# Seven strips of a convolution layer: small steps of a norm and a count moved behind the first half of the strip's vertical sums

## The chip, the core and the metric

The kernel runs on one core of a Trainium2 chip. The metric is the device time of one execution in microseconds; lower is better. All tensors are 32-bit floats. Engines are named as in the profile: PE (TensorE, matrix products, writes to PSUM), DVE (VectorE), ACT (ScalarE), POOL (GpSimd) and SP (SyncE, which here only issues DMAs).

## The reference

Two layers, each of the form x + conv(groupnorm(x)), on x of shape (2, 128, 256, 256). Layer 0's "convolution" is a dilated halo attention over 8x8 windows. Layer 1, to which the change belongs, is

```python
t1 = conv(x, w1, 5x1 kernel, padding 2 rows)        # 128 channels to 128, along the rows
t3 = depthwise conv(t1, w3, 3x1 kernel, padding 1)
t2 = unfold(x, width taps 0, 2, 4)                  # dilated by 2 along the columns
t4 = einsum('nckhw,ckg->nghw', t2, w4)              # g = 8
t5 = t4[:, None] * t3.reshape(n, c // g, g, h, w)
x  = x + t5
```

The group norm ahead of it has 32 groups of 4 channels and needs mean and variance over the whole image before the first row can be normalised.

## The kernel before

The 128 channels lie on the 128 partitions. Both layers go through the image in strips of 8 rows: 32 strips an image, 64 in all, numbered k. Layer 0 (`attention_fast`) writes its result x1 to device memory, strip by strip, and collects the statistics of x1 for layer 1's norm on the way. Layer 1 (`convolutions_fast`, L607) starts when layer 0 ends.

Two small pieces of work are left over when layer 1 starts. **The norm of image 1** (`Norms.steps`, L115): the statistics of its last strips come at the very end of layer 0, so its mean and reciprocal deviation are computed inside layer 1, in seven steps, each ended by a `yield`: `bn_aggr` on DVE (L119); a matmul `pm` that averages over each group (L122); the mean and three one-column operations on DVE (L125 to L130); a matmul `pv` (L133); one DVE operation (L136); a square root on ACT (L139); five one-column DVE operations (L143 to L148). They are needed only when the second image starts, at strip 31. **The count** (`in_range`, L882): one reduction and a memset on DVE in its first part, one matmul `total` and a cast on DVE in its second. It says whether all softmax denominators were in range; a slower program behind it would run if they were not.

A strip k of layer 1, in program order:

- `load_rows1(k + 2)` (L629): SP issues the loads of x1's rows for the strip after the next into `raw` (six buffers).
- `unfold(k)` (L686): 12 matmuls of PE from the normalised rows `xm` into `g` (L692), copied to SBUF by ACT (L698).
- `first_rows(k)` (L709): ACT carries two rows of `t1` over (L723).
- `start_strip(k + 1)` (L666), which calls `normalise1`: ACT copies the four rows that two strips share (L649); DVE normalises the new eight (L651).
- `vertical(k, 2)` (L727): the 5x1 convolution for half of the strip, in the form of sums and differences of rows: matmuls `a_c` (L706, called from L735), copied by ACT into `both` (L737); `a_d` (L740), added to `both` by DVE into `c` (L744); `a_e` (L706) and `a_o` (L706), added to `c` by DVE (L751 and L757) into `t1`; then ACT starts `t3` (L762). `a_c`, `a_d`, `a_e` and `a_o` rotate through three PSUM buffers, so each needs the one three places back to have been read.
- `row_sums(k + 1)` (L670): ACT carries over one row of `sm` (L677); DVE makes the row sums `sm` (L678) and their differences `df` (L682), which the next strip's `a_c` and `a_d` read.
- `depthwise(k, 2)` (L764): two DVE operations on `t3` (L769).
- `vertical(k, 4)`: the other half, in the same way.
- `spread(k)` (L774): four matmuls into four PSUM banks of one buffer each, b0 to b3 (L780).
- `combine` (L786) on DVE: `y` = bank times `t3`, for b0 and b1; then `depthwise(k, 4)`; then b2 and b3 (L789).
- `finish(k)` (L794): POOL issues a DMA that adds x1 to `y` (L797); SP issues the store of `y` (L798), which waits for it.

The small matmuls `total`, `pm` and `pv` use the tag "b3", so each takes the bank that `combine` of strip k − 1 reads last and that `spread(k)` writes next.

The order is written out by hand: inside `tc.manual_schedule(engines=ORDERED)` each engine, and SP's queue, runs its instructions in the order of the program, and semaphores are put in where one depends on another. So an instruction that waits holds up everything after it on its engine. The loop is at L819; the steps stand in it at L827 to L832:

```python
if k in (1, 2):
    count_good[k - 1](ps_b, "b3")
if k == 2:
    steps = norm.steps(st_y[NB - 1], ps_b, f"y{NB - 1}", "b3")
for _ in range({3: 1, 4: 2, 5: 2, 6: 1, 7: 1}.get(k, 0)):
    next(steps)
```

That is: strip 1 the reduction of the count, strip 2 its matmul and cast, strip 3 `bn_aggr`, strip 4 `pm` and the mean, strip 5 `pv` and the operation after it, strip 6 the square root, strip 7 the rest.

Of the kernel before, what the change touches and what calls it, by code (L numbers as in the profile page):

```python
# [606 lines left out]
def convolutions_fast(tc, io, x1_d, norm, st_y, out, weights, count_good):  # L607
# [4 lines left out]
    with ExitStack() as l1:  # L612
# [16 lines left out]
        def load_rows1(b, s):  # L629

            if s == 0:
                pre = rawp.tile([P, 8, W], F32, tag="raw", name=f"raw1_{b}_pre")
                nc.sync.dma_start(pre[:, 5:8, :], x1_d[b][0][:, 0:3, :])
                raws[b, -1] = pre
            t = rawp.tile([P, 8, W], F32, tag="raw", name=f"raw1_{b}_{s}")
            nc.sync.dma_start(t[:, 0:5, :], x1_d[b][s][:, 3:8, :])
            if s + 1 < NS:
                nc.sync.dma_start(t[:, 5:8, :], x1_d[b][s + 1][:, 0:3, :])
            raws[b, s] = t

        def normalise1(b, s, k, mean, rstd):
            cur, prev = xn[k % 2], xn[(k + 1) % 2]
            if s == 0:
                nc.gpsimd.memset(cur[:, 0:1, :], 0.0)
                nc.vector.tensor_scalar(
                    cur[:, 1:4, 2 : 2 + W], raws[b, -1][:, 5:8, :], mean, rstd, ALU.subtract, ALU.mult
                )
            else:
                nc.scalar.copy(cur[:, 0:4, :], prev[:, 8:12, :])  # L649
            n = 8 if s + 1 < NS else 5  # L650
            nc.vector.tensor_scalar(  # L651
                cur[:, 4 : 4 + n, 2 : 2 + W], raws[b, s][:, 0:n, :], mean, rstd, ALU.subtract, ALU.mult
            )
            if n < 8:
                nc.gpsimd.memset(cur[:, 4 + n : 12, :], 0.0)
# [10 lines left out]
        def start_strip(k):  # L666
            b, s = divmod(k, NS)
            normalise1(b, s, k, *norm.done[f"y{b}"])

        def row_sums(k):  # L670
            s = k % NS
            xt = xn[k % 2]
            sms[k] = sm = tp.tile([P, 5, W], F32, tag="sm", name=f"sm_{k}")
            dfs[k] = df = tp.tile([P, 4, W], F32, tag="df", name=f"df_{k}")
            lo = 0 if s == 0 else 1
            if s > 0:
                nc.scalar.copy(sm[:, 0:1], sms[k - 1][:, 4:5])  # L677
            nc.vector.tensor_tensor(  # L678
                sm[:, lo:5], xt[:, 2 * lo + 1 : 10 : 2, 2 : 2 + W], xt[:, 2 * lo + 2 : 11 : 2, 2 : 2 + W],
                ALU.add,  # L680
            )
            nc.vector.tensor_tensor(df, sm[:, 0:4], sm[:, 1:5], ALU.subtract)  # L682
# [3 lines left out]
        def unfold(k):  # L686

            xt = xn[k % 2]
            pg = ps_pj.tile([P, 512], F32, tag="pj", name=f"g_{k}")
            for tap in range(3):  # L690
                for j in range(4):
                    nc.tensor.matmul(  # L692
                        pg[32 * j : 32 * j + 32, :], w4[:, tap, :],
                        xt[:, 2 * j + 1 : 2 * j + 3, 2 * tap : 2 * tap + W],
                        start=tap == 0, stop=tap == 2,
                    )
            t4 = wk.tile([P, 512], F32, tag="t4", name=f"t4_{k}")
            nc.scalar.copy(t4, pg)  # L698
            t3 = wk.tile([P, 8, W], F32, tag="t3", name=f"t3_{k}")
            y = wk.tile([P, 8, W], F32, tag="y", name=f"y_{k}")  # L700
            ts[k] = t4, t3, y

        def taps(name, n, terms):
            pa = ps_a.tile([P, 512], F32, tag="a", name=f"a_{name}")
            for i, (w, rows) in enumerate(terms):
                nc.tensor.matmul(pa[:, : n * W], w, rows, start=i == 0, stop=i == len(terms) - 1)  # L706
            return pa[:, : n * W].rearrange("p (r w) -> p r w", w=W)

        def first_rows(k):  # L709

            s = k % NS
            xt = xn[k % 2]

            t1s[k] = t1 = tp.tile([P, 10, W], F32, tag="t1", name=f"t1_{k}")
            if s == 0:
                nc.gpsimd.memset(t1[:, 0:1, :], 0.0)
                top = taps(
                    f"{k}_first", 1,
                    [(w1[:, tap], xt[:, tap - 1 : tap, 2 : 2 + W]) for tap in (2, 3, 4)],
                )  # L720
                nc.scalar.copy(t1[:, 1:2, :], top)
            else:
                nc.scalar.copy(t1[:, 0:2, :], t1s[k - 1][:, 8:10, :])  # L723
            if s + 1 == NS:
                nc.gpsimd.memset(t1[:, 9:10, :], 0.0)

        def vertical(k, m):  # L727

            s = k % NS
            xt, sm, df, t1 = xn[k % 2], sms[k], dfs[k], t1s[k]  # L730

            def rows(j):
                return xt[:, j : j + 3 : 2, 2 : 2 + W]

            pa = taps(f"{k}_c_{m}", 1, [(w1s[:, 0], sm[:, m - 1 : m])])  # L735
            both = wk.tile([P, 1, W], F32, tag="both", name=f"both_{k}_{m}")
            nc.scalar.copy(both, pa)  # L737
            pa = ps_a.tile([P, 512], F32, tag="a", name=f"a_{k}_d_{m}")
            for i, w in enumerate((w1[:, 1], w1s[:, 1])):
                nc.tensor.matmul(  # L740
                    pa[:, W * i : W * i + W], w, df[:, m - 2 + i : m - 1 + i], start=True, stop=True
                )
            c = wk.tile([P, 2, W], F32, tag="c", name=f"c_{k}_{m}")
            nc.vector.tensor_tensor(  # L744
                c, pa.rearrange("p (r w) -> p r w", w=W), both.to_broadcast([P, 2, W]), ALU.add
            )
            pa = taps(
                f"{k}_e_{m}", 2,
                [(w, rows(2 * m - 4 + 2 * i)) for i, w in enumerate((w1[:, 0], w1s[:, 2], w1s[:, 3]))],
            )  # L750
            nc.vector.tensor_tensor(t1[:, 2 * m - 2 : 2 * m + 1 : 2, :], pa, c, ALU.add)  # L751
            pa = taps(
                f"{k}_o_{m}", 2,
                [(w, rows(2 * m - 3 + 2 * i)) for i, w in enumerate((w1s[:, 4], w1s[:, 5], w1[:, 4]))],
            )
            n = 1 if m == 4 and s + 1 == NS else 2
            nc.vector.tensor_tensor(  # L757
                t1[:, 2 * m - 1 : 2 * m + 2 * n - 2 : 2, :], pa[:, 0:n], c[:, 0:n], ALU.add
            )
            t3 = ts[k][1]  # L760
            j = 2 * m - 4
            nc.scalar.activation(t3[:, j : j + 4], t1[:, j : j + 4, :], AF.Copy, scale=w3[:, 0:1])  # L762

        def depthwise(k, m):  # L764

            t1, t3 = t1s[k], ts[k][1]
            j = 2 * m - 4
            for tap in (1, 2):
                nc.vector.scalar_tensor_tensor(  # L769
                    t3[:, j : j + 4], t1[:, j + tap : j + tap + 4, :], w3[:, tap : tap + 1],  # L770
                    t3[:, j : j + 4], ALU.mult, ALU.add,
                )
# [41 lines left out]
        with tc.manual_schedule(engines=ORDERED):  # L814
            for k in range(2):
                load_rows1(*divmod(k, NS))
            start_strip(0)
            row_sums(0)
            for k in range(NB * NS):  # L819
                more = k + 1 < NB * NS  # L820
                if k + 2 < NB * NS:
                    load_rows1(*divmod(k + 2, NS))
                unfold(k)
                first_rows(k)


                if k in (1, 2):  # L827
                    count_good[k - 1](ps_b, "b3")
                if k == 2:
                    steps = norm.steps(st_y[NB - 1], ps_b, f"y{NB - 1}", "b3")  # L830
                for _ in range({3: 1, 4: 2, 5: 2, 6: 1, 7: 1}.get(k, 0)):
                    next(steps)  # L832
                if more:
                    start_strip(k + 1)

                vertical(k, 2)
                if more:
                    row_sums(k + 1)
                depthwise(k, 2)
                vertical(k, 4)  # L840
                banks = spread(k)
                combine(k, banks, (0, 1))
                if not more:
                    finish_half(k, 0)
                depthwise(k, 4)
                combine(k, banks, (2, 3))
                if more:
                    finish(k)
                else:
                    finish_half(k, 1)  # L850
# [596 lines left out]
```

## Time and profile before

| What | us |
|---|---|
| Median of 3 runs | 3231.89 (3228.91 to 3233.07) |
| The profiled execution, its time | 3226.79 |
| The profiled execution, its span | 3224.9 |
| PE busy in the span | 3084.4 (96%) |
| DVE busy | 2611.7 (81%) |
| ACT busy | 1440.3 (45%) |
| POOL busy | 586.7 (18%) |
| PE busy in 2100 to 3225 us (layer 1) | 1092.15 of 1125 |
| DVE busy in the same | 975.16 |

The span is from the first to the last instruction of the profiled execution; its time has a little around that. A row of the profile names the line, the engine, what is written and read, how often, the busy time and the mean of one; "idle before" is time in which the engine stood still just before such an instruction, and the name after the arrow is what ended it. Wait rows have the total, the number of times and the longest. PE, the costliest engine, runs matmuls in a pipeline, so consecutive rows overlap a little in the timeline. In layer 1 a first row at about 2104 us is the first `unfold`, and strip 1 starts at 2129.32 us.

### The profile page before, as it was taken

How to read it: one execution, taken by the hardware profiler on the slowest of the kernel's cores; microseconds unless marked ns; L12 is line 12 of the kernel's file. 1: busy time of each engine (PE TensorE's matmuls, PEld its weight loads, DVE VectorE, ACT ScalarE, POOL GpSimd, SP SyncE). 2: the span in 40 equal slices, each digit the busy share in tenths (PEclk: the TensorE clock that was granted, in tenths of full speed). 3: DMA queues.
4: the chain of work that ended last, by engine and by line, in shares of the span. 5: the costliest groups of instructions: out<-in, count | busy, mean ns of one | idle time of the engine just before them, and what ended most of it. 6: DMA issues, size and time to landing. Idle time of an engine off the chain costs nothing.

```text
span 3224.9 us, 117425 instructions
## 1 busy us (share of the span) xinstructions
PE 3084.4 (96%) x53030; PEld 2282.9 (71%) x53030; DVE 2611.7 (81%) x4152; ACT 1440.3 (45%) x2481; POOL 586.7 (18%) x917
## 2 busy tenths in 40 slices
PE   0799999999999999999999999989999999999998
PEld 0688898899988889988998889834444444444443
DVE  8788888888888777777777777678888898888887
ACT  0455555555555555555555555522332323233322
POOL 2222222222222222222222222100000000000001
PEclk9999999999999999999999999999999999999999
DMA  9443333333333222222222222146677767676775
GB/s 396 148 133 111 122 108 111 110 120 119 107 111 99 81 75 80 85 68 86 80 78 85 68 88 81 40 135 160 187 194 182 185 186 190 178 190 186 194 182 153
DMA packets 125116, 426.42 MB, mean 132 GB/s; under 512 B 9024, under 2 KB 75328, under 8 KB 92096
## 3 DMA queue, kind: packets, MB, share of 16 engines
q1 hardware_dynamic: 115536, 352.76, 32.2%
q0 software_dynamic: 9072, 66.06, 11.3%
q8 instruction: 420, 6.88, 0.9%
q14 instruction: 88, 0.72, 0.1%
HBM read 284.57 MB, written 134.22 MB: 130 GB/s over the span
## 4 chain that ended last, share of the span: by engine, by line
PE 76%; issue 18%; DVE 2%; POOL 2%; DMA 1%; ACT 0%; SPq 0%; POOLq 0%; DVEq 0%; ACTq 0%
PE f_pv L416 15%; PE f_pq L341 8%; PE f_s L451 8%; PE f_o L476 8%; PE f_pk L341 7%; PE f_py L341 7%; PE a_e L706 5%; PE a_o L706 5%; PE f_pa L395 4%; PE f_s L435 4%; PE g L692 3%; PE a_d L740 2%; POOL y L797 1%; PE b L780 1%; PE a_c L706 1%
## 5 line engine op out<-in xcount | busy, mean ns | idle before, releaser
L422 DVE COPY f_vt<-f_pv 64x512 f32<-64x512 f32 x512 | 354.3, 694 | 291.6 <-ACT f_vt L422 291.4
L416 PE MATMUL f_pv<-f_wqkvT,f_xn 128*128 128x128 f32 x4096 | 491.4, 278 | 0.0
L416 PEld LDWEIGHTS f_pv<-f_wqkvT,f_xn 128*128 128x128 f32 x4096 | 466.9, 192 | 8.6
L762 ACT ACTIVATE t<-t,w 128x1024 f32<-128x1024 f32 x128 | 147.2, 1150 | 689.0 <-DVE t L757 689.0
L323 POOL COPY f_xq<-f_xn 128x256 f32<-128x256 f32 x512 | 309.7, 649 | 757.8 <-DVE f_xn L309 757.8
L376 ACT ACTIVATE f_q<-f_pq,f_head 128x512 f32<-128x512 f32 x512 | 309.9, 687 | 304.2 <-PE f_pq L341 304.2
L460 ACT ACTIVATE f_p<-f_s 128x512 f32<-128x512 f32 x512 | 264.3, 603 | 404.1 <-PE f_s L451 404.0
L422 ACT COPY f_vt<-f_pv 64x512 f32<-64x512 f32 x512 | 297.4, 582 | 118.0 <-PE f_pv L416 117.8
L769 DVE SCALAR_TENSOR_TENSOR t<-t,w,t 128x1024 f32<-128x1024 f32 x256 | 329.9, 1289 | 7.5 <-ACT t L762 1.3
L451 PEld LDWEIGHTS f_s<-f_q,f_kt 64*64 64x64 f32 x16384 | 250.6, 135 | 49.3 <-issue 49.3
L341 PE MATMUL f_pq<-f_xn,f_wq_s 128*128 128x192 f32 (+2 forms) x1520 | 277.2, 330 | 3.3 <-DVE f_xn L309 2.6
L451 PE MATMUL f_s<-f_q,f_kt 64*64 64x64 f32 x16384 | 268.2, 220 | 0.0
L476 PE MATMUL f_o<-f_vt,f_p 128*32 128x66 f32 x16384 | 265.3, 223 | 0.9 <-DVE mean_x L125 0.3
L797 POOL DMA_DIRECT2D y<-f_x x63 | 71.3, 1131 | 1025.1 <-DVE y L789 960.7
L476 PEld LDWEIGHTS f_o<-f_vt,f_p 128*32 128x32 f32 x16384 | 243.2, 111 | 10.5 <-DVE f_cf L408 1.0
L341 PE MATMUL f_pk<-f_xn,f_wqkvT 128*128 128x256 f32 x1024 | 245.3, 380 | 0.0
L341 PEld LDWEIGHTS f_pq<-f_xn,f_wq_s 128*128 128x128 f32 x1520 | 232.3, 188 | 17.0 <-issue 4.2
L341 PE MATMUL f_py<-f_ot,f_woT 128*128 128x256 f32 x1024 | 241.8, 378 | 2.3 <-DVE f_ot L494 2.3
L706 PE MATMUL a_e<-xm,w1s 128*128 128x512 f32 x512 | 240.7, 591 | 0.0
L706 PE MATMUL a_o<-xm,w1s 128*128 128x512 f32 x512 | 240.5, 590 | 0.0
L300 POOL COPY f_xn<-f_xn 128x1280 f32<-128x1280 f32 x62 | 86.5, 1395 | 772.1 <-PE f_pv L416 772.1
L510 DVE TENSOR_TENSOR f_x<-f_py,f_raw 128x512 f32<-128x512 f32 x256 | 175.9, 687 | 58.7 <-PE f_py L341 50.7
(126 smaller groups left out, 4612.6 us busy)
## 6 DMA issues: line engine op xcount, KB each, us to landing
f_raw<-in_x SPq DMA_DIRECT2D x62, 1280.0 KB, 7.8
f_sx<-in_x SPq DMA_DIRECT2D x64, 1024.0 KB, 7.3
f_x<-f_x SPq DMA_DIRECT2D x128, 512.0 KB, 3.3
y<-f_x POOLq DMA_DIRECT2D x63, 1024.0 KB, 8.2
out<-y SPq DMA_DIRECT2D x63, 1024.0 KB, 4.9
raw<-f_x SPq DMA_DIRECT2D x64, 640.0 KB, 6.4
raw<-f_x SPq DMA_DIRECT2D x62, 384.0 KB, 6.9
f_raw<-in_x SPq DMA_DIRECT2D x2, 1024.0 KB, 6.9
```

Source lines behind the costliest of these rows:

```text
L323: nc.gpsimd.tensor_copy(xq[:, t2, half].rearrange("p t r n c e -> p r t (n c) e"), cells[:, :, 16 * half : 16 * half + 16, 1 + t2 : 9 : 4, ...
L341: nc.tensor.matmul(dst[:, 32 * lo : 32 * hi], w, moving[:, lo:hi], start=True, stop=True)
L376: nc.scalar.activation(q[:, c, :, i], pq.rearrange("p (n x) -> p n x", n=NPAIR), AF.Copy, scale=head[:, i : i + 1],)
L416: nc.tensor.matmul(pv[:, P * n : P * n + P], xn[k % 2][:, r, 4 * j + n].rearrange("p c x -> p (c x)"), wvT, start=True, stop=True,)
L422: (nc.vector.tensor_copy if c else nc.scalar.copy)(vt[rows, 4 * j : 4 * j + 4, :, c, 0:32], pv[rows].rearrange("p (n h d) -> p n h d", n=4 ...
L451: nc.tensor.matmul(sc[g][n // 8][64 * c : 64 * c + 64, n % 8].rearrange("p i x -> p (i x)"), keys_k[rows, c, 48 * n : 48 * n + 64], qs[u][ ...
L460: nc.scalar.activation(pts[u][:, g, 8 * half : 8 * half + 8].rearrange("p n i x -> p (n i x)"), sc[g][half].rearrange("p n i x -> p (n i x ...
L476: nc.tensor.matmul(po[32 * h : 32 * h + 32, n - lo], p[:, h // 2, n, h % 2], vt[:, n, h], start=True, stop=True,)
L510: nc.vector.tensor_tensor(x1[:, :, c:W:2], py.rearrange("p (m t) -> p t m", t=4), raws[k][:, r:8:2, c:W:2], ALU.add,)
L706: nc.tensor.matmul(pa[:, : n * W], w, rows, start=i == 0, stop=i == len(terms) - 1)
L762: nc.scalar.activation(t3[:, j : j + 4], t1[:, j : j + 4, :], AF.Copy, scale=w3[:, 0:1])
L769: nc.vector.scalar_tensor_tensor(t3[:, j : j + 4], t1[:, j + tap : j + tap + 4, :], w3[:, tap : tap + 1], t3[:, j : j + 4], ALU.mult, ALU.add,
```

## The change

The six lines above move from between `first_rows(k)` and `start_strip(k + 1)` to between `vertical(k, 2)` and `row_sums(k + 1)`. In the file it looks as if the two calls moved up; the order of everything else stays. Strips in which no step is run have the same order before and after.

```diff
                 unfold(k)
                 first_rows(k)
+                if more:
+                    start_strip(k + 1)
+
+                vertical(k, 2)
 
 
                 if k in (1, 2):
                     count_good[k - 1](ps_b, "b3")
                 if k == 2:
                     steps = norm.steps(st_y[NB - 1], ps_b, f"y{NB - 1}", "b3")
                 for _ in range({3: 1, 4: 2, 5: 2, 6: 1, 7: 1}.get(k, 0)):
                     next(steps)
-                if more:
-                    start_strip(k + 1)
-
-                vertical(k, 2)
                 if more:
                     row_sums(k + 1)
                 depthwise(k, 2)
```

## The prediction

> **What bounds the kernel now.** I read the page first: PE is busy 96% of the span and makes 76% of the chain that ended last. The edit touches layer 1 only, from about 2100 us on, so I asked next for the busy time of stretches of that layer (columns: PE, PE loads, DVE, ACT, POOL, then granted clock, DMA share, GB/s).
>
> ```profile
> 2166.40:2185.60 19.20, 17.37 (x72) 7.50 (x68) 18.36 (x19) 5.20 (x8) 0.86 (x1) 1.00 0.60 159
> 2185.60:2207.50 21.90, 18.86 (x74) 8.96 (x70) 15.73 (x22) 5.29 (x8) 0.86 (x1) 0.92 0.64 181
> 2300.00:2900.00 600.00, 600.00 (x2409) 274.09 (x2408) 533.29 (x604) 182.50 (x282) 43.69 (x40) 1.00 0.71 185
> ```
>
> From 2300 us PE never rests (600.00 of 600), with DVE at 89%: PE sets the pace there. Only the first strips leave PE idle. The waits of PE in layer 1 say why:
>
> ```profile
> PE g L692 <- issue: 5.4, 1, 5.4
> PE total L893 <- DVE y L789: 3.1, 1, 3.1
> PE pv_y L133 <- DVE y L789: 3.1, 1, 3.1
> PE pm_y L122 <- DVE y L789: 3.0, 1, 3.0
> PE g L692 <- DVE xm L651: 2.6, 1, 2.6
> PE a_c L706 <- DVE c L744: 2.1, 2, 1.7
> ```
>
> The two rows of g are the start of the layer, untouched. The three of 3.1, 3.1 and 3.0 are the small matmuls of the count and the norm. Their target is PSUM bank b3, and DVE reads b3 last of all in the strip before (combine, L789). The timeline around the first, PE (columns: start, us, engine, line, what):
>
> ```profile
> 2146.21 2.79 PE L692 MATMUL g<-xm,w 128*32 128x512 f32 x24
> 2152.07 0.19 PE L893 MATMUL total<-ones,both 128*1 128x1 f32 x2 [3.08 <-DVE y L789]
> 2152.19 0.70 PE L706 MATMUL a_c<-sm,w1s 128*128 128x256 f32 x2
> ```
>
> and DVE, whose last read of b3 is the second of these two:
>
> ```profile
> 2150.73 1.29 DVE L789 TENSOR_TENSOR y<-b,t 128x512 f32<-128x512 f32 x2
> ```
>
> PE is through with unfold at 2149.00; DVE leaves b3 at 2152.02. In strip 1, with no small matmul, PE goes straight from g (ends 2132.11) to a_c (2132.04, overlapped), while DVE is just as far behind (y ends 2135.15).
>
> **Strip by strip.** Unfold (L692) starts, in the timeline, for k = 1 to 10: 2129.32, 2146.21, 2166.36, 2185.61, 2207.52, 2227.76, 2244.81, 2261.68, 2279.53, 2296.48. An undisturbed strip is 16.88. Excess over that: k=2 3.27, k=3 2.37, k=4 5.03, k=5 3.36, k=6 0.17, k=7 0, k=8 0.97, k=9 0.07; together 15.2 us, the ceiling.
>
> **What the Trainium skill says.** "PSUM — Partial Sum Buffer", Engine vs sequencer instructions: matmuls run in program order, the other engines' queues are FIFO. The trace agrees: all of vertical stood behind the waiting `total` for 3.08 us. "TensorE: Matmul & The Clock Gate", What's actually happening: PE's clock falls to half after an idle window of 3413 ns, and windows run freely. The 0.92 above is one: in 2191 to 2196 us the mean clock is 0.66, so (1 − 0.66) × 5 / 0.5 = 3.4 us at half speed, costing 1.7. It follows one of the three waits and not the other two of the same length. "ScalarE: Activation LUTs", What ACT_TABLE_LOAD costs: 1283 ns and about 1380 of drain. The trace shows 1.28 and no drain: load 2231.75, square root 2233.04, the next copy 2233.15, so I take 1.4.
>
> **The change part by part.** Strips without steps (0, 8 and later) keep their order. In 1 to 7 the steps now stand after vertical(k, 2), still ahead of row_sums.
>
> *Count, strips 1 and 2.* In strip 2 the matmul comes after a_o, which in strip 1 ends 6.7 us after the strip's first a_c (2138.76 against 2132.04), when b3 has been free for 3.6 us. The wait of 3.08 and its refill go: 3.27 − 0.12 for the matmul itself (2152.07 to 2152.19) = **3.15**. DVE's cast needs that matmul, 0.28 behind it before; DVE has o's add (L757, 0.69) to do first, so it waits for nothing. The reduction and memset (0.13 of DVE in strip 1) lie in DVE's slack: it waited 0.86 for a_o there. If that cover were gone they cost 0.13.
>
> *pm and pv, strips 4 and 5.* Likewise, leaving 0.24 each (2191.45 to 2191.69). The half clock goes with the wait, as no idle window of that length is left in these strips. Strip 5: 3.36 − 0.24 = **3.1**. Strip 4: 5.03 − 0.24 = **4.8**, of which 1.7 is clock. The four small operations behind pm are 0.66 of DVE; in their place and after o's add, 0.44 of that lies in DVE's old wait for ACT's sm copy (L677), which is waited for in every strip.
>
> *bn_aggr, strip 3.* DVE, 3.61 long:
>
> ```profile
> 2172.07 3.61 DVE L119 BATCH_NORM_AGGREGATE mv_y<-st_y 128x2 f32<-128x768 f32 x1
> 2175.60 1.28 DVE L651 TENSOR_SCALAR xm<-raw,mean_y,rstd_y 128x2048 f32<-128x2048 f32 x1
> 2177.53 0.70 PE L706 MATMUL a_c<-sm,w1s 128*128 128x256 f32 x2 [1.73 <-DVE c L744]
> 2269.46 1.35 DVE L651 TENSOR_SCALAR xm<-raw,mean_y,rstd_y 128x2048 f32<-128x2048 f32 x1 [1.96 <-DMA raw<-f_x]
> ```
>
> It does not vanish; it becomes late somewhere else. I need a rule for how late DVE may be. Vertical(k, 4) takes buffers that DVE's adds of vertical(k, 2) free, and these follow normalise (L651). In strip 3 normalise starts 6.52 after the first a_c (2175.60 − 2169.08) and the strip has 2.37 excess; in strip 8 it starts 5.05 after (2269.46 − 2264.41), with 0.97 excess. Both give: PE stalls by what normalise is later than 4.1 after the first a_c. An ordinary strip has 3.1, so 1.0 us of slack. After the change: bn_aggr adds 3.53, less 0.44 (the sm wait) = 3.1, to the second half of strip 3. There the nearest limit is the e add against the next strip's a_d, 3.3 us of room (the add starts at 2145.51 and ends at 2146.2 in strip 1; a_d would stand at 2149.5 without the wait), so no stall yet. Strip 4's normalise then starts at 3.1 + 3.1 = 6.2 and PE stalls 6.2 − 4.1 = 2.1. So strip 3's 2.37 is won and **2.1 given back** in strip 4. After that DVE is 1.0 late and regains about 1.1 per strip (15.77 from one normalise to the next in strip 8, against 16.88).
>
> *Square root, strip 6.* It now stands ahead of the sm copy and `both` on ACT. df waits for the copy: 1.4 later, none of it covered, as DVE there already waits 0.44. y ends 1.4 late, normalise in strip 7 starts at 4.5: stall **0.4**, for the 0.17 that strip 6 loses now. Bounds: 0 if DVE has caught up, 1.4 if it has no slack.
>
> *Last step, strip 7.* Five operations, 0.84, of which 0.44 in the sm wait; the rest in slack: 0.
>
> *Queues.* No step issues a DMA. Only SP's early read of `good` depends on them: about 4.6 us later, near 2157 by the old times, before the store at 2161.00 that follows it on SP. The accumulating load on POOL (L797) now has normalise directly after y, as in strip 1, where it took 1.21; in strip 7, beside the small operations, 1.90.
>
> *DMA.* Loads of strip k+2 stand on SP behind the store of strip k−1, which waits for the accumulating load. From the end of y to loaded rows: 9.0 to the store, 0.9 to the load, 6.9 to landing, 16.8 in strips 1 to 3; 18.9 once (2250.60 to 2269.46). Late loads cost PE nothing up to 16.88 + 1.0 = 17.9. One such cost 0.97 in strip 8 before; I take half of it, 0.5, after.
>
> *Sum.* Left over: 2.1 + 0.4 + 0.12 + 0.24 + 0.24 + 0.5 = 3.6. Gain 15.2 − 3.6 = **11.6 us**. From 2300 us on PE is the bound without a gap, so the gain arrives at the end. The profiled execution (span 3224.9, time 3226.79) becomes 3215.2; the three runs' median of 3231.89, which lies 5.1 above the profiled one, becomes **3220.3**, 0.36% less. A change within 0.2%, 6.5 us, is about what the measurement can't tell from none: faster means below 3225.4, slower above 3238.4.
>
> **Rivals.** *The loads were hidden under the waits.* Strips 2 to 5 lasted about 20 us; at 16.88 a load taking 18.9 as that one did stalls each of strips 3 to 8 by 1.0: 6 × 1.0 instead of 0.5 gives back 5.5, so 3225.8, on the border. For: 13 waits for loads in the layer, 13.9 us. Against: 16.8 in these strips, and PE without a gap at 16.88 later. *The wait only moves.* PE would run 3.06 on and meet DVE at the second a_c; 9.2 come back and the rest is 2.4: 3229.5, no change. Against: strip 1 has the same distance and no stall. *More half-speed windows.* The executions above the profiled one may hold a second one; then 1.7 to 3.4 more goes: about 3217.5. *Slower:* an earlier start shifts accumulating loads against stores, and the chain of loads passes 17.9 in the 56 later strips too; at 0.35 us each that is 19.6, and 3220.3 + 19.6 = 3240. It decides from a mean of 18.25 per load chain; the 13 waits averaging 1.1 in 62 strips speak against it.
>
> **How the numbers follow.** Forecast 66% (3220.3, alone 3218 to 3223.5); hidden loads 14%, half of it on each side of the border; moved wait 7%; more windows 10%; slower 3%. Faster 0.66 + 0.10 + 0.07 = 0.83, same 0.07 + 0.07 = 0.14, slower 0.03. The range leaves out the moved wait and slower: 3216.5 to 3227.
>
> **What would show it.** Right: no PE wait on L789 in strips 2, 4 and 5; strip lengths of about 17.0, 16.9, 19.2, 17.1, 16.9 and 17.3 for k = 2 to 7; one stall of some 2 us at strip 4's second a_c or a_d, on DVE; ACT's table load followed by a late df in strip 6; no half clock near 2190. Wrong: DMA ahead of L651 in several of strips 3 to 8, a_c waiting in strips 2 and 5, or PE gaps after 2300.

## The result and the profile after

| | before | after |
|---|---|---|
| Median of 8 runs, us | 3229.36 (3226.22 to 3234.93) | 3217.03 (3214.89 to 3221.29) |
| The profiled execution, us | 3226.79 | 3215.36 |
| Its span | 3224.9 | 3213.6 |

The ratio is 0.9961, with a 95% interval of 0.995 to 0.9972: 0.39% faster; the medians differ by 12.3 us. The profiled executions differ by 11.4 us, with a forecast of 11.6.

The waits of PE in layer 1, after its first strip (columns: who waited on whom, us in total, times, longest):

```profile
PE a_c L706 <- DVE c L744: 1.1, 2, 0.7
PE a_o L706 <- ACT both L737: 0.5, 2, 0.3
```

The three rows with L789 are gone. What is left is an `a_c` that waits for `c` in strip 4 (0.71) and in strip 8 (0.36), and two short waits for ACT. The timeline of PE where `total` now stands:

```profile
2154.06 1.02 PE L706 MATMUL a_o<-xm,w 128*128 128x512 f32 x2
2155.01 0.19 PE L893 MATMUL total<-ones,both 128*1 128x1 f32 x2
2155.13 0.70 PE L706 MATMUL a_c<-sm,w1s 128*128 128x256 f32 x2
```

It runs without a gap between `a_o` and the next `a_c`. DVE is no faster than before: it ends strip 1's last read of b3 at 2151.45, 3.0 us after PE's unfold of strip 2 (2148.43); that time is now filled with `vertical`. The busy time of strips 3 and 4 and of the part where PE sets the pace:

```profile
2162.84:2179.73 16.89, 16.89 (x73) 7.70 (x69) 15.27 (x15) 5.21 (x8) 1.46 (x1) 1.00 0.75 196
2179.73:2198.66 18.93, 17.83 (x74) 7.75 (x71) 18.18 (x25) 5.08 (x8) 1.08 (x1) 1.00 0.58 149
2300.00:2900.00 600.00, 599.90 (x2429) 272.54 (x2428) 533.95 (x605) 183.79 (x282) 40.59 (x39) 1.00 0.71 188
```

Strip 3 has no gap left (16.89 of 16.89), strip 4 has one of about 1.1, and the granted clock is 1.00 in both, where strip 4 had 0.92. The long stretch is as it was.

The measure that I use from here is the length of a strip, from one start of unfold to the next in the profiled execution, less the 16.88 of an ordinary strip. It can be read to 0.02 us, but each row is one execution. In strips 2 to 9 the kernel before and the one with 20 more waits (below) run the same program; there they agree within 0.1. The medians can't tell so little apart:

| Excess, us | k=2 | 3 | 4 | 5 | 6 | 7 | 8 | 1 to 9 |
|---|---|---|---|---|---|---|---|---|
| before | 3.27 | 2.37 | 5.03 | 3.36 | 0.17 | 0 | 0.97 | 15.2 |
| forecast for after | 0.12 | 0 | 2.34 | 0.24 | 0 | 0.4 | 0.5 | 3.6 |
| after | 0.32 | 0.01 | 2.05 | 0.23 | 0.75 | 0.01 | 0.99 | 4.4 |
| bank b0, nothing moved | 0.02 | 2.37 | 0.23 | 0.23 | 0.16 | 0 | 1.03 | 4.1 |
| only the matmul steps moved | 0.31 | 2.06 | 0.23 | 0.23 | 0.16 | 0.02 | 0.92 | 4.0 |
| only the other steps moved | 3.26 | 0 | 9.66 | 5.04 | 0.49 | 0 | 1.07 | 19.5 |
| after, bn_aggr in strip 0 | 0.33 | 0 | 0.24 | 0.24 | 0.17 | 0 | 0.42 | 1.4 |
| after, loads three ahead | 0.33 | 0.01 | 2.05 | 0.23 | 0.49 | 0 | 0.01 | 3.1 |
| all that helped | 0.01 | 0 | 0.23 | 0.23 | 0.16 | 0 | 0.01 | 0.7 |

So 15.2 − 4.4 = 10.8 us of the 11.4 come from these strips. The rest was there before strip 1 started (2128.75 against 2129.32), which the edit does not touch.

### The profile page after: what moved, and what is told of

Same layout as the page of the kernel before. It is cut to its first block, busy times and chain, and to the rows that moved or that the text cites. A ratio compares the mean times of both kernels' runs of the same rounds, so it can differ in the third digit from the quotient of the medians.

```text
span 3213.6 us, 117425 instructions
## 1 busy us (share of the span) xinstructions
PE 3081.7 (96%) x53030; PEld 2280.1 (71%) x53030; DVE 2611.1 (81%) x4152; ACT 1439.9 (45%) x2481; POOL 584.8 (18%) x917
## 4 chain that ended last, share of the span: by engine, by line
PE 85%; issue 10%; DVE 2%; DMA 1%; POOL 1%; ACT 0%; SPq 0%; POOLq 0%; DVEq 0%; ACTq 0%
PE f_pv L416 15%; PE f_pq L341 8%; PE f_s L451 8%; PE f_o L476 8%; PE a_e L706 7%; PE a_o L706 7%; PE f_pk L341 7%; PE f_py L341 7%; PE f_pa L395 4%; PE f_s L435 4%; PE g L692 4%; PE a_d L740 3%; PE b L780 2%; PE a_c L706 1%; DMA raw<-f_x 1%
```

## The experiments

My theory was that PE's wait for bank b3 is the whole gain, and that bn_aggr and the square root only change the strip in which they cost. The rivals: that DVE gains by having its normalise and its adds ahead of the steps; that the loads were hidden under the waits; that a wait is taken back later.

**Another bank, nothing moved.** In the kernel before, the steps stay in their place and only their bank changes.

```diff
-                    count_good[k - 1](ps_b, "b3")
+                    count_good[k - 1](ps_b, "b0")
...
-                    steps = norm.steps(st_y[NB - 1], ps_b, f"y{NB - 1}", "b3")
+                    steps = norm.steps(st_y[NB - 1], ps_b, f"y{NB - 1}", "b0")
```

> The kernel before, with nothing moved: the three small matmuls only take PSUM bank b0 in place of b3. DVE reads b0 about 4 us earlier than b3, so that PE should not wait. My theory (the gain is the wait of PE for bank b3): no wait of PE on L789 in strips 2, 4 and 5; excess over 16.88 us a strip, in strips 1 to 9: 0.3 (k=2), 2.4 (k=3, bn_aggr where it was), 0.25 (k=4), 0.25 (k=5), 0.2 (k=6), about 1.0 (k=8), together 4.3 as in the changed kernel (4.4); time about 3217 to 3218. Rival (the gain comes from DVE normalising and adding ahead of the steps): the excess stays above 12 and the time above 3226, as DVE's order is the old one.

Measured: 3216.07 us (6 runs), ratio 0.9966 (0.9953 to 0.9978); the excess is 4.1, both a little below what I had expected. Every wait of PE from strip 1 on:

```profile
PE a_c L706 <- DVE c L744: 2.1, 2, 1.7
```

The order of DVE is that of the kernel before and the whole gain is there. The rival about DVE's order falls. `pm` in strip 4 with its neighbours shows a small matmul in its old place that waits for nothing, as its bank is free; it costs 0.23 here, as it does in the new place:

```profile
2183.05 2.79 PE L692 MATMUL g<-xm,w 128*32 128x512 f32 x24
2185.77 0.38 PE L122 MATMUL pm_y<-mv_y,f_gavg 128*128 128x1 f32 x2
2186.01 0.68 PE L706 MATMUL a_c<-sm,w1s 128*128 128x256 f32 x2
```

**One half of the change, and the other.** First only the steps that hold a matmul are moved, in the kernel before (a cut in the code is marked with dots):

```diff
-                if k in (1, 2):
-                    count_good[k - 1](ps_b, "b3")
+                if k == 1:
+                    count_good[0](ps_b, "b3")
                 if k == 2:
                     steps = norm.steps(st_y[NB - 1], ps_b, f"y{NB - 1}", "b3")
-                for _ in range({3: 1, 4: 2, 5: 2, 6: 1, 7: 1}.get(k, 0)):
+                for _ in range({3: 1, 6: 1, 7: 1}.get(k, 0)):
                     next(steps)
...
                 vertical(k, 2)
+                if k == 2:
+                    count_good[1](ps_b, "b3")
+                for _ in range({4: 2, 5: 2}.get(k, 0)):
+                    next(steps)
```

> One part alone: only the steps with a matmul (the count's second part in strip 2, pm and pv with the DVE operations after them in strips 4 and 5) are moved behind the first vertical; bn_aggr, the square root and the last step stay where they were. My theory: the three waits go and bn_aggr costs 2.4 in strip 3 instead of 2.05 in strip 4, the square root 0.2 instead of 0.75: excess 4.3, time as the changed kernel, 3217 to 3218. Rival (bn_aggr's move brings its share of the gain): excess near 6.5 or more, time about 3220.

Measured: 3216.55 us (6 runs), ratio 0.9967 (0.9955 to 0.998), excess 4.0: all of the gain. bn_aggr costs 2.06 in strip 3 in its old place (2.37 in the two kernels above, where normalise starts 6.5 us after the strip's first a_c and not 6.2 as here) and 2.05 − 0.23 = 1.8 in strip 4 in its new one.

Then the same two groups the other way round, with the matmuls in front and the rest behind.

> The other part alone: bn_aggr, the square root, the reduction and the last step are moved, the three matmuls stay in front. My theory: bn_aggr's lateness is not seen in strip 3 but lengthens the wait for bank b3 in strip 4 to about 6.2 us, so the part alone brings nothing: excess 3.3, 0, 6.5 (8.2 with a half clock), 3.4, 0.75, 0, 1.0 for k = 2 to 8, together 15 to 16.7 against 15.2 before; time 3229 to 3231. Rival (the DVE work's place is what counts): 2 to 5 us faster than before, 3224 to 3227.

Measured: 3231.15 us (20 runs), ratio 1.0008 (1.0001 to 1.0014): not faster, and slower by a hair, just over the 3229 to 3231 that I had expected. The wait for b3 in strip 4 took in what bn_aggr made late, as expected, and the clock then took more than I had allowed. The timeline of PE there:

```profile
2194.62 0.58 PE L122 MATMUL pm_y<-mv_y,f_gavg 128*128 128x1 f32 x2 [6.20 <-DVE y L789]
2195.06 1.20 PE L706 MATMUL a_c<-sm,w1s 128*128 128x256 f32 x2
2196.06 1.06 PE L740 MATMUL a_d<-df,w 128*128 128x256 f32 x2
```

The wait is 6.20, and `a_d` after it takes 1.06, where it takes 0.59 at full clock. The half clock lasts 10.24 us here, some of it in the wait itself, and a second one of 3.41 falls in strip 5: 9.66 and 5.04 in the table where I had 6.5 to 8.2 and 3.4.

**bn_aggr where DVE waits anyway.** In strip 0, after start_strip(1), DVE waits 3.5 us for ACT's first `both`. The statistics are complete by then.

```diff
+                if k == 6:
+                    next(steps)
                 if more:
                     start_strip(k + 1)
+                if k == 0:
+                    steps = norm.steps(st_y[NB - 1], ps_b, f"y{NB - 1}", "b3")
+                    next(steps)
 
                 vertical(k, 2)
...
-                if k == 2:
-                    steps = norm.steps(st_y[NB - 1], ps_b, f"y{NB - 1}", "b3")
-                for _ in range({3: 1, 4: 2, 5: 2, 6: 1, 7: 1}.get(k, 0)):
+                for _ in range({4: 2, 5: 2, 7: 1}.get(k, 0)):
```

> The changed kernel, with bn_aggr in strip 0 between start_strip and the first vertical, where DVE waits 3.5 us for ACT, and the square root back in front of start_strip. My theory: bn_aggr is covered by that wait, strip 4 loses its stall and strip 6 its 0.75: excess 0.3, 0, 0.25, 0.25, 0.2, 0, 1.0 = 2.0 in place of 4.4, time 2.4 less than the changed kernel, about 3214.7, and strip 0 no longer than before by more than 0.2. Rival (DVE's wait in strip 0 is the path itself, or the rest is DMA): strip 0 becomes longer by up to 3.5 and the time is 3218 or more.

Measured: 3214.36 us (5 runs), ratio 0.9956 (0.9941 to 0.997); excess 1.4 where I had expected 2.0, as strip 8 has 0.42 and not 1.0. DVE in strip 0:

```profile
2112.09 1.34 DVE L651 TENSOR_SCALAR xm<-raw,mean_y,rstd_y 128x2048 f32<-128x2048 f32 x1
2113.34 3.62 DVE L119 BATCH_NORM_AGGREGATE mv_y<-st_y 128x2 f32<-128x768 f32 x1
2118.36 0.69 DVE L744 TENSOR_TENSOR c<-a_d,both 128x512 f32<-128x512 f32 x1 [1.41 <-ACT both L737]
```

bn_aggr is covered: DVE still waits 1.41 for ACT behind it. Strip 4's stall and half a microsecond of strip 6 are gone. Strip 0 itself, counted from the row of unfold that waited for its first `xm` (2109.06 before, 2109.44 here), has an excess of 4.2, 0.8 more than before, outside the 0.2 that I had allowed. This is no cost of bn_aggr: the 0.8 lies ahead of the first a_c, where PE waits for nothing but has a mean clock of 0.57 (7.04 us long), before 0.66 (6.20 us); from there to strip 1 it takes 14.05, before 14.06. In the last experiment, with bn_aggr in the same place, strip 0 has 2.6. Against the changed kernel the medians differ by 2.7 and the intervals overlap; the strips say it, the time alone does not.

**Loads three strips ahead,** in the changed kernel.

```diff
-                if k + 2 < NB * NS:
-                    load_rows1(*divmod(k + 2, NS))
+                for i in (2, 3) if k == 0 else (k + 3,):
+                    if i < NB * NS:
+                        load_rows1(*divmod(i, NS))
```

> The changed kernel, with the loads of raw issued three strips ahead in place of two, so that a load no longer stands behind the store of the strip just ended. The stall of strip 8 (0.97 before, 0.99 after, 0.9 to 1.1 in three of the four experiments so far) is a late load by my reading. My theory: strip 8 has no excess any more, DVE's waits for raw (15 times, 15.4 us) shrink to those at the start of the layer (about 4 to 6 us), excess of strips 1 to 9 is 3.4 in place of 4.4, time about 3216, which the time alone can't tell from the changed kernel. Rival (the load is late because the DMA engines are full, not because of its place in SP's queue): strip 8 keeps 0.9 or more and the waits stay above 12 us.

Measured: 3214.83 us (4 runs), ratio 0.995 (0.9935 to 0.9965), 1.2 below the expected time; excess 3.1. DVE's waits for `raw` in layer 1, in the changed kernel:

```profile
DVE xm L651 <- DMA raw<-f_x: 15.4, 15, 3.7
```

and with the loads earlier:

```profile
DVE xm L651 <- DMA raw<-f_x: 2.8, 1, 2.8
```

Only the first load of the layer is waited for, and strip 8 has no excess. So its 0.97 was a late load, and one strip more of lead covers it. The run does not tell the load's place in SP's queue from a slow landing, since a load that is issued a strip earlier still stands behind a store and may also land late. The trace shows both parts: the load that strip 8 waits for landed 8.1 us after its issue in the kernel before and 8.2 after the change, where 6.8 is usual there, and the slow one at about the same time here took 8.7 and cost nothing. Strip 6 falls from 0.75 to 0.49, as its normalise had been late by a load too (1.49).

**Twenty more waits, at the old place and at the new.** `total` and its cast are repeated in strips 10 to 29, in the kernel before and in the changed one; nothing else changes.

```diff
-                if k in (1, 2):
-                    count_good[k - 1](ps_b, "b3")
+                if k in (1, 2) or 10 <= k < 30:
+                    count_good[min(k, 2) - 1](ps_b, "b3")
```

> The kernel before, with the count's second part (matmul into bank b3 and cast) repeated in strips 10 to 29 at its old place: 20 more of the suspected wait. My theory: each of the 20 waits about 3.1 us for L789 and lengthens its strip by 3.27, 65 us in all, and some of them bring a half clock of 1.7 on top (one in three did): time 3228.5 + 65 + 11 = about 3305, from 3294 to 3328. Rival (a wait this long is taken back later, as DVE and DMA catch up meanwhile): less than 2 us per strip, below 3270.

> The changed kernel, with the same 20 repeats at the new place, behind the first vertical. My theory: no wait for L789; each costs the 0.32 that strip 2 has over 16.88, 6.4 us in all: about 3223.5, with no half clock in strips 10 to 29. Rival (the wait only hides while DVE has slack, and 20 in a row wear it out): waits for L789 or stalls at the second a_c come back, 1 us or more per strip, above 3237.

Measured at the old place: 3318.86 us (2 runs), ratio 1.0274 (1.0256 to 1.0293). The medians differ by 88.7 us; in the trace the 20 strips have 92.0 us excess: 8 have 3.26 to 3.29, 6 about 4.86 and 6 about 6.1. The first value is the bare wait; the others have a half clock of 3.41 or 6.83 us on top. PE's waits in these strips:

```profile
PE total L893 <- DVE y L789: 61.5, 20, 3.1
```

and the 20 strips as a whole, with a mean clock of 0.93:

```profile
2299.00:2729.00 430.00, 368.53 (x1408) 171.49 (x1408) 306.15 (x362) 105.96 (x160) 30.95 (x20) 0.93 0.57 149
```

At the new place: 3223.09 us (20 runs), ratio 0.998 (0.9973 to 0.9987); 0.31 to 0.34 per strip, no wait for L789 and no half clock in these strips. Twenty in a row do not wear out DVE's slack, and a wait is not taken back later. (One other stall stands out in this execution, 1.82 in strip 41, where DVE waited 2.8 for a load.) The same small matmul costs 92.0 / 20 = 4.6 us in one place and 0.32 in the other.

**All that helped:** the steps in front, as in the kernel before, but with bank b0; bn_aggr in strip 0; loads three ahead.

```diff
-                if k + 2 < NB * NS:
-                    load_rows1(*divmod(k + 2, NS))
+                for i in (2, 3) if k == 0 else (k + 3,):
+                    if i < NB * NS:
+                        load_rows1(*divmod(i, NS))
...
                 if k in (1, 2):
-                    count_good[k - 1](ps_b, "b3")
-                if k == 2:
-                    steps = norm.steps(st_y[NB - 1], ps_b, f"y{NB - 1}", "b3")
-                for _ in range({3: 1, 4: 2, 5: 2, 6: 1, 7: 1}.get(k, 0)):
+                    count_good[k - 1](ps_b, "b0")
+                for _ in range({4: 2, 5: 2, 6: 1, 7: 1}.get(k, 0)):
                     next(steps)
                 if more:
                     start_strip(k + 1)
+                if k == 0:
+                    steps = norm.steps(st_y[NB - 1], ps_b, f"y{NB - 1}", "b0")
+                    next(steps)
```

> What the runs point to, together: the steps in front of start_strip as in the kernel before, but with bank b0; bn_aggr in strip 0 under DVE's wait; the loads three strips ahead. My theory: excess 0, 0, 0.23, 0.23, 0.16, 0, 0 for k = 2 to 8, 0.7 in all against 4.4 after the change and 1.4 with bn_aggr early alone: 3213 to 3214. Rival (the earlier loads or bank b0 collide with something else): above 3215.

Measured: 3212.24 us (5 runs), ratio 0.9947 (0.9934 to 0.9961), a little under the 3213 to 3214 expected. It beats the kernel before by 0.53%. Beside the changed kernel (0.9961, 0.995 to 0.9972) the intervals overlap, so the last 4.8 us of the medians are not separated by the times; the trace has 3.7 of them, 4.4 − 0.7.

## Why the prediction was right

- **The three waits.** Forecast 3.15, 4.8 and 3.1 for strips 2, 4 and 5. Measured: 3.27 − 0.32 = 2.95 and 3.36 − 0.23 = 3.13; strip 4, where bn_aggr's stall now lies, went from 5.03 to 2.05. The bank experiment shows strip 4 alone: 5.03 − 0.23 = 4.80.
- **The residue of `total`** was mis-sized: 0.12 forecast, 0.32 measured, and again in each of the 20 repeats. In front of the first `a_c`, with a free bank, it costs 0.02. In the changed kernel's timeline the step from the `a_c` behind `total` to `a_d` is 0.53, where one inside a strip is 0.43; I had counted the row itself and not what it does to its neighbours; the step from a_o over `total` to a_c is longer too, 1.07 where 0.86 is usual.
- **The half clock** went with the waits, as forecast: none in strips 2 to 9 after. That it follows from them is shown by the 20 repeats, with 12 half clocks at the old place and none at the new. Which of the three waits of equal length brought it depends on where each lies in time (last section), so that 1.7 of the gain may be absent in another execution. The rate was mis-sized in the expectation of that run: one in three by the three waits of before, 12 in 20 measured, which is most of why that run lies above its 3305.
- **bn_aggr** was given back in the next strip as forecast: 2.1 forecast, 2.05 − 0.23 = 1.8 measured, in strip 4. The rule used for it, stall = normalise later than 4.1 us after the strip's first a_c, gives 2188.59 − 2182.45 − 4.1 = 2.0 there. The rule also fits late strips that it was not made from: 6.21 gave 2.06 (only the matmul steps moved, strip 3) and 4.50 gave 0.42 (bn_aggr in strip 0, strip 8). PE waited 0.29 of it at a_o, for ACT's `both`, and 0.71 at a_c. The rest lies in the matmuls next to these waits, whose starts are further apart: from a_c to a_d 0.80, where it is 0.51 in strip 5 behind `pv`. What makes them so is not shown.
- **The square root** had about the right size and the wrong place. Forecast: df late, so y late, so 0.4 in strip 7. Measured: 0.75 in strip 6 itself and 0.01 in strip 7; 0.49 and 0 without late loads. ACT after the change:

```profile
2227.44 1.28 ACT L139 ACT_TABLE_LOAD   x1
2228.74 0.20 ACT L139 ACTIVATE sd_y<-v_y 128x1 f32<-128x1 f32 x1
2228.85 0.39 ACT L677 COPY sm<-sm 128x256 f32<-128x256 f32 x1
2229.14 0.36 ACT L737 COPY both<-a_c 128x256 f32<-128x256 f32 x1
```

  The price of 1.4 holds (2227.44 to 2228.85). df did wait for it (1.94 where 0.44 is usual). But `both` stands behind it too, and a_o of the second half needs the buffer that `both` reads: PE waited there, 0.20. I followed the first reader on the queue and not the second. The other 0.26 of the 0.75 is the late load by the rule above: normalise started 4.36 after the first a_c, 0.26 over the rule's 4.1. With strip 6 longer, strip 7's first a_c came later too, and its normalise started 4.02 after it where I had 4.5, just within the rule.
- **Loads.** Forecast half of strip 8's 0.97, measured 0.99. It is not chance: the strip showed 0.9 to 1.1 in seven kernels with loads two strips ahead and 0.42 in an eighth. After the change 1.4 of the 1.49 that its normalise waits is the slow landing (8.2 against 6.8). What makes that load land late each time stays open; with loads three ahead it costs nothing. The rival that loads would take half of the gain in strips 3 to 8 is refuted by the table: strips 3, 5 and 7 have 0.01 to 0.23.
- **SP's read of `good`** was placed wrong: at 2162.7, behind the store and the loads of that strip, not ahead of them near 2157. It cost nothing that the trace shows.
- **The base.** The sum was made against the profiled execution and gave 3215.2; the profiled one after took 3215.36. The median of before in the prediction, 3231.89 of 3 runs, was 2.5 above that of 8 runs, and that is most of the distance from 3220.3 to 3217.03. The rival with more half-speed windows, at 3217.5, lies nearer to this median than the forecast; with one trace of each kernel the record can't tell what such windows gave in the other executions. That the profiled one was met within 0.2 is luck in part: the strips gave 10.8 where the sum had 11.6, and 0.6 came from ahead of strip 1, which the sum did not contain. One reading was off, with nothing resting on it: strip 10 starts at 2296.41, not 2296.48, so strip 9 has no excess.

## What to carry to other kernels

A small matmul in an ordered program is priced by the bank it writes, not by its 0.2 us: ask who reads that bank last and how far that engine is behind PE. Either put the matmul after enough work to cover the distance, or give it a bank that is read earlier; the second did as much here with the order unchanged. A long operation on an engine with about 1 us of slack per strip is not hidden by moving it within the strip, since the lateness comes out one strip on; it needs a place where its engine already waits that long.

## What the runs showed of the hardware that I had not expected

- PE gaps of 3.07 us, shorter than one stretch at half clock (3.41), brought half clocks in 12 of 20 strips, of 3.41 and 6.83 us in turn, in a pattern that came again every three strips; the gap of 6.20 brought 10.24. The dearest strips cost 6.1 us for a gap of 3.07. Where a gap lies in time decides. In each of the ten traces the clock changes, through layer 1, only on a grid of 3.413 us. From strip 1 to 3180 us, each of the 16 windows of that grid at full clock in which PE was busy for up to 0.38 of the time was followed by one at half clock, and none in which it was busy for 0.42 or more; at half clock, windows of up to 0.88 were followed by another, and those of 0.96 or more were the last. So a window need not be idle throughout, as the prediction had it. A gap that fills most of one window is dear, and the same gap cut near its middle by a window's end costs only itself. Three strips of the repeats take 64.85 us, 19 windows, so the pattern repeats. Windows around a gap that brought 6.83 us, and around one that brought none (the first number after the length is PE's busy time, the one near the end the clock):

```profile
2361.26:2364.67 3.41, 1.14 (x12) 0.13 (x4) 3.25 (x4) 2.18 (x4) 0.00 (x0) 1.00 0.05 18
2364.67:2368.08 3.41, 2.61 (x8) 2.11 (x9) 2.18 (x4) 0.37 (x1) 1.53 (x1) 0.50 0.13 14
2368.08:2371.50 3.42, 3.42 (x6) 1.47 (x5) 0.69 (x1) 0.00 (x0) 0.00 (x0) 0.50 0.88 170
2405.63:2409.05 3.42, 1.61 (x16) 0.26 (x8) 3.26 (x5) 2.33 (x4) 0.00 (x0) 1.00 0.00 0
2409.05:2412.46 3.41, 2.16 (x10) 1.71 (x11) 3.00 (x5) 0.69 (x2) 1.53 (x1) 1.00 0.00 0
```

- Strip 0 varies by itself: in the eight kernels whose edits leave its work on PE, DVE and ACT as it was, its excess is 2.75 to 3.71 us in the profiled executions, with half clocks of 10 to 17 us in all around the start of the layer. That is as much as some of the differences between the better versions, and why the strips from 1 on and not the medians tell them apart.
